# A state-space block on one core: sums over states and x*D turned in quarters of 32 channels, with one PSUM bank for each quarter

## The chip, the cores and the metric

The kernel runs on one core of a Trainium2 chip. The metric is the device time of one execution in microseconds (us); lower is better. Three executions of the kernel before took 2848.3, 2849.82 and 2853.23 us; their median, 2849.82 us, is what the changed kernel is compared with.

The engines have short names here: PE is TensorE's matmul row and PEld its weight loads, DVE is VectorE, ACT is ScalarE, POOL is GpSimd, and SP (SyncE) issues most of the DMAs.

## What is computed

The input x has 8 sequences of 2048 tokens of 512 channels, in fp32. A selective state-space layer with 16 states is added to x, and then a linear layer whose inputs are rounded to 8 bits. Cut to what matters:

```python
n = layernorm(x)
xp = n @ x_proj_w.T                       # 64 ranks, 16 B, 16 C
delta = softplus(xp[..., :64] @ dt_proj_w.T + dt_proj_b)
h[t] = exp(delta[t] * A) * h[t-1] + delta[t] * B[t] * n[t]   # per channel and state
y[t] = sum over the 16 states of h[t] * C[t]
x1 = x + y + n * D
z = layernorm(x1); zq = round(z / scale_of_row)
out = x1 + (zq @ weight_q.T) * scale_of_row * weight_scale + bias
```

## The kernel before, in words

The tokens are cut into 32 chunks of 512 (four chunks make one sequence). Within a chunk the kernel goes through 16 states, and within a state through the four groups `d` of 128 channels; one such step is a slot, so a chunk has 64 slots. Channels lie on the partitions while states are scanned along time, and tokens lie on the partitions before and after.

For each state of a chunk:

- ACT makes the decay `da` (line 742) and, for 10 of the 16 states, the product `bT` of delta*n with B, with tokens on the partitions (line 772). `b_pe` turns bT with transposes on PE (line 795). For the other six states a diagonal matrix with B on it is loaded from DRAM, and PE multiplies with it (line 786), which scales and turns at once.
- DVE runs the scan over 512 tokens, four to a state (line 804), reading `pb` from PSUM.
- POOL multiplies the state's result by C, 128 x 2048 elements in one instruction (line 830), giving `hc`.
- PE turns hc back to tokens and adds it to `y` in PSUM: `y_pe` and `y_halves` (lines 841 to 869). Each block of 128 channels x 128 tokens is turned as two products, one of partitions 0 to 63 and one of 64 to 127. In each, 64 rows of hc (128 columns) are the weights, and a 64 x 64 piece of the identity is the moving operand. A state has 16 blocks, so 32 such products.

Three things go into the same sums y. `skip_pe` (line 875) adds n*D with products against a diagonal of D, also in halves. `add_x` (line 580) adds the input x with the whole identity as weights, in two products of 256 columns. The state sums themselves accumulate over the whole chunk.

PSUM has eight banks. y takes four of them, as two tiles of two banks: tile `y0` holds token blocks 0 and 1, `y1` blocks 2 and 3. In each, one bank belongs to channel half 0 and the other to half 1, so that two products that run side by side write different banks. Three banks hold `pb` (tag "b") and one is for everything else (`misc`).

When a chunk's sums are complete, `residual` (line 611) copies y of each token block to SBUF on ACT (line 612), and the layer norm, the rounding and the quantized product of that chunk run in between the next chunk's states. y of the next chunk takes the same banks, so its first products wait for those copies.

The order on every engine is written out by hand. `pin` keeps instructions in program order, and `PREP_AT`, `POST_AT`, `LATE_AT`, `SKIP_AT` and `LAST_ADD_X` give a slot to each step. A chunk's last state sum stands in slot 7 of the next chunk, its last two add_x in slot 10, its four copies in slots 12, 12, 13 and 14, and the next chunk's first two state sums in slot 15. The transposes of bT run two slots ahead of the scans, bT and the decay about two states ahead. SP's queue carries the loads of x, of C (line 820) and of the diagonals (line 767).

At the start, 16 products of the identity with itself (line 507) keep PE working until the first tokens are normalised; then tokens are turned (line 456), projected (line 470) and taken to delta (lines 487 and 499), with `pdt` in the two y tiles. At the end, `finish` sums the last state channel group by channel group, copies y out (line 1003) and does the quantized product, with its output `po` (line 981) in the y tiles in turn.

Of the kernel before, what the change touches and what calls it, by code (L numbers as in the profile page):

```python
# [9 lines left out]
F32 = mybir.dt.float32  # L10
# [4 lines left out]
ALU = mybir.AluOpType  # L15
AX = mybir.AxisListType

P = 128
HALF = 64
T = 512  # L20
LN_EPS = 1e-05
Q_EPS = 1e-06
# [80 lines left out]
def kernel(  # L103
# [13 lines left out]
    nc = tc.nc  # L117
# [6 lines left out]
    ND = DM // P  # L124
    NT = T // P
    G = 4
    NG = N // G
    NPAIR = N // 2
    CPB = L // T
    NCHUNK = B * CPB  # L130
    assert OUT == T == DM

# [11 lines left out]
    ps_y = ctx.enter_context(tc.tile_pool(name="ps_y", bufs=1, space=bass.MemoryType.PSUM))  # L144
# [3 lines left out]
    pin = tc.keep_in_program_order  # L148
# [17 lines left out]
    ident = const.tile([P, P], F32, name="ident")  # L166
# [11 lines left out]
    pin(nc.sync.dma_start(out=dtproj_sb[:R], in_=dtproj_t))  # L178
    xp = const.tile([P, T], F32, name="xp")
    pin(nc.gpsimd.memset(xp, 0.0))  # L180
    dtb_sb = const.tile([P, ND], F32, name="dtb_sb")
    pin(nc.sync.dma_start(out=dtb_sb, in_=dt_b.rearrange("(c p) -> p c", p=P)))
    dsk_sb = const.tile([P, ND], F32, name="dsk_sb")
# [4 lines left out]
    pin(nc.sync.dma_start(out=wq_i32, in_=wq_t.rearrange("(c p) o -> p c o", p=P)))  # L188
    zeros = work.tile([P, T], F32, tag="hc", bufs=3, name="zeros")
    pin(nc.vector.memset(zeros, 0.0))  # L190
# [5 lines left out]
    diag_d = const.tile([P, ND, P], F32, name="diag_d")  # L196
# [23 lines left out]
    def gpsimd_constants():  # L220

        for d in range(ND):
            pin(
                nc.gpsimd.tensor_scalar(
                    diag_d[:, d, :], ident, dsk_sb[:, d : d + 1], None, ALU.mult
                )
            )
        pin(nc.gpsimd.tensor_copy(wq_sb, wq_i32.bitcast(I8)))
# [7 lines left out]
    das, pbs, bts, hs, hcs, ys = {}, {}, {}, {}, {}, {}  # L236
# [39 lines left out]
    def misc(name):  # L276
        return ps_m.tile([P, T], F32, tag="ps", name=name)

# [137 lines left out]
    def prep_first(second):  # L416
# [11 lines left out]
        bt = chan.tile([P, NT, N], F32, tag="BT", name="BT_0")  # L428
        b_t[0] = bt
        pts, pps = {}, {}  # L430

        def measure(i):
            st = small.tile([P, 6], F32, tag="st", name=f"st_0_{i}")
            pin(nc.vector.bn_stats(st, x[:, i, :]))
            pin(nc.vector.bn_aggr(mv[:, i, :], st))
            one = slice(i, i + 1)
            pin(nc.vector.tensor_scalar(ve[:, one], mv[:, i, 1:2], LN_EPS, None, ALU.add))
            pin(nc.gpsimd.tensor_tensor(rstd[:, one], ve[:, one], nhalf[:, one], ALU.pow))
# [41 lines left out]
        def dt(i):  # L480
            for d in range(ND):
                if i == 0:
                    if d % 2 == 0:
                        pdt = ps_y.tile([P, 2, T], F32, tag=f"y{d // 2}", name=f"pdt_0_{d // 2}")
                    pps[d] = pdt[:, d % 2, :]
                pin(
                    nc.tensor.matmul(
                        pps[d][:, ts(i, P)],
                        lhsT=dtproj_sb[:, ts(d, P)],
                        rhs=xp[:, ts(i, P)],  # L490
                        start=True,
                        stop=True,
                    )
                )
# [7 lines left out]
            )  # L502


        pw = misc("pwarm")
        for _ in range(16):
            pin(nc.tensor.matmul(pw[:, :P], lhsT=ident, rhs=ident, start=True, stop=True))
        measure(0)
        measure(1)
        norm(0)  # L510
# [44 lines left out]
        for s in range(2):  # L555
            bts[s] = work.tile([P, NT, P], F32, tag="dg", bufs=2, name=f"dg_0_{s}")
            for i in range(NT):
                pin(
                    nc.gpsimd.tensor_scalar(
                        bts[s][:, i, :], ident, bt[:, i, s : s + 1], None, ALU.mult  # L560
                    )
                )
        for d in range(ND):
# [4 lines left out]
            t = x[:, :, ts(d, P)]  # L568
            pin(nc.vector.tensor_tensor(t, pt.rearrange("p (i d) -> p i d", d=P), t, ALU.mult))
        b_pe(0)  # L570
        b_pe(1)
        plan(0, [(1, step) for step in second[3:]])
        gpsimd_constants()
        zero_diagonals(0)
        store_diagonals(0)
# [4 lines left out]
    def add_x(k, i):  # L580

        t = split(x1[k, i // 2][:, i % 2, :])
        for half in range(2):
            pin(
                nc.tensor.matmul(  # L585
                    ys[k, i // 2][:, half, i % 2, :, :],
                    lhsT=ident,
                    rhs=t[:, :, half, :],
                    start=False,
                    stop=False,  # L590
                    skip_group_check=True,
                )
            )

    def split(t):
        return t.rearrange("p (d h c) -> p d h c", h=2, c=HALF)

    def post(k):

# [241 lines left out]
    def y_pe(s):  # L841

        if s < 0 or s >= LAST - 1:
            return
        k, n = divmod(s, N)
        for i in range(NT):
            if n == 0 and i % 2 == 0:
                ys[k, i // 2] = ps_y.tile(  # L850
                    [P, 2, 2, ND, HALF], F32, tag=f"y{i // 2}", name=f"y_{k}_{i // 2}"
                )
            for d in range(ND):
                y_halves(k, i, d, hcs[s], first=(n == 0 and i % 2 == 0 and d == 0))

    def y_halves(k, i, d, hc, first=False, last=False):
        for half in range(2):
            rows = ds(half * HALF, HALF)
            pin(
                nc.tensor.matmul(  # L860
                    ys[k, i // 2][:, half, i % 2, d, :],
                    lhsT=hc[rows, d, ts(i, P)],
                    rhs=ident[rows, rows],
                    is_transpose=True,
                    start=first,
                    stop=last,
                    skip_group_check=True,
                )
            )

    def y_of(k, i):

        return ys[k, i // 2][:, :, i % 2, :, :].rearrange("p h d c -> p d h c")

    def skip_pe(k, i):

        for d in range(ND):
            for half in range(2):
                rows = ds(half * HALF, HALF)
                pin(  # L880
                    nc.tensor.matmul(  # L881
                        ys[k, i // 2][:, half, i % 2, d, :],
                        lhsT=xn_t[k][rows, d, ts(i, P)],
                        rhs=diag_d[rows, d, rows],
                        start=False,
                        stop=False,
                        skip_group_check=True,
                    )
                )

    def finish():


        k, s = NCHUNK - 1, LAST - 1
        h = hs.pop(s)
        hc = work.tile([P, ND, T], F32, tag="hc", bufs=3, name=f"hc_{k}_{N - 1}")
        c = cts.pop(s)
        for d in range(ND):
            pin(nc.vector.tensor_tensor(hc[:, d, :], h[:, d, :], c, ALU.mult))  # L899
            for i in range(NT):  # L900
                y_halves(k, i, d, hc, last=(d == ND - 1))
        mv = small.tile([P, NT, 2], F32, tag=f"mv{NT}", name="mv_last")
        am = small.tile([P, NT], F32, tag="am", name="am_last")
        xs = small.tile([P, NT], F32, tag="xs", name="xs_last")
# [8 lines left out]
        st = {}  # L913
# [27 lines left out]
        pw = misc("pwarm_last")  # L941
# [29 lines left out]
        def turned(i):  # L971
            qt = work.tile([P, ND, P], BF16, tag="qT", name=f"qT_last_{i}")
            pin(
                nc.scalar.activation(
                    qt,
                    st["pz", i].rearrange("p (d t) -> p d t", t=P),
                    AF.Copy,
                    bias=-ROUND,
                )
            )  # L980
            po = ps_y.tile([P, 2, T], F32, tag=f"y{i % 2}", name=f"po_last_{i}")[:, 0, :]
            for d in range(ND):
                pin(
                    nc.tensor.matmul(
                        po, lhsT=qt[:, d, :], rhs=wq_sb[:, d, :], start=(d == 0), stop=(d == ND - 1)
                    )
                )
            st["po", i] = po
# [23 lines left out]
        measure(3)  # L1012
        norm(2)
        turned(0)
        largest(1)
        rounded(1)
        norm(3)
        turned(1)
        for i in range(NT):
            pin(nc.gpsimd.tensor_tensor(x1_of(i), x1_of(i), bias_b, ALU.add))  # L1020
# [25 lines left out]
    for k in range(NCHUNK):  # L1046
        plan(k * SLOTS, [(SKIP_AT[i], lambda k=k, i=i: skip_pe(k, i)) for i in range(NT)])
        if k < NCHUNK - 1:
            plan((k + 1) * SLOTS, post(k))
        if k + 1 < NCHUNK:  # L1050
            plan(k * SLOTS, [at for at in prep_of[k + 1] if at[0] >= 0 or k > 0])
    want = 0
    for u in range(NCHUNK * SLOTS + Y_BEHIND):
        k, slot = divmod(u, SLOTS)
        s, d = divmod(u, ND)
# [28 lines left out]
        if k == NCHUNK - 1 and slot in LAST_LOAD:  # L1084
            j = LAST_LOAD.index(slot)
            t = work.tile([P, 2, DM], F32, tag="x1", bufs=3, name=f"x1_{k}_{j}")
# [53 lines left out]
```

## Time and profile before

| what | value |
|---|---|
| three executions | 2848.3, 2849.82, 2853.23 us |
| median | 2849.82 us |
| span of the profiled execution | 2848.6 us |
| instructions in it | 80379 |
| first chunk's stretch, 0 to 71 us: POOL busy | 44.60 us |
| line 860 weight loads | 16384, mean 139 ns |
| line 881, x*D | 2048 records, mean 275 ns |
| line 585, residual on PE | 512 records, mean 381 ns |
| ACT copies of y, line 612 | 124, median 588 ns |

The profile is of one execution. Its span of 2848.6 us runs from the first to the last instruction of the program; no other time is given for that execution, and it lies 1.2 us below the median.

In a row of the groups the columns are: line, engine, operation, output<-inputs, shapes and count, then busy time and mean duration in ns, then the idle time of the engine just before, and what ended it. A matmul's duration is from its start to a modelled end and includes the passage through the array; products overlap, so the distance between starts tells what one more product costs, and the busy time doesn't. An fp32 product that isn't a transpose has two records, for its two passes. In a timeline, rows of one group are merged: start, length of the whole group, and xN. A timeline of a narrow window counts the instructions that touch that window.

### The profile page before, as it was taken

How to read it: one execution, taken by the hardware profiler on the slowest of the kernel's cores; microseconds unless marked ns; L12 is line 12 of the kernel's file. 1: busy time of each engine (PE TensorE's matmuls, PEld its weight loads, DVE VectorE, ACT ScalarE, POOL GpSimd, SP SyncE). 2: the span in 40 equal slices, each digit the busy share in tenths (PEclk: the TensorE clock that was granted, in tenths of full speed). 3: DMA queues.
4: the chain of work that ended last, by engine and by line, in shares of the span. 5: the costliest groups of instructions: out<-in, count | busy, mean ns of one | idle time of the engine just before them, and what ended most of it. 6: DMA issues, size and time to landing. Idle time of an engine off the chain costs nothing.

```text
span 2848.6 us, 80379 instructions
## 1 busy us (share of the span) xinstructions
PE 2739.1 (96%) x33032; PEld 2357.2 (83%) x33032; DVE 2731.4 (96%) x2949; ACT 2723.7 (96%) x4762; POOL 2771.5 (97%) x1243
## 2 busy tenths in 40 slices
PE   8999999999999999999999999999999999999988
PEld 6888888888888888888888888888888878888877
DVE  6999999999999999999999999999999999999998
ACT  7999999999999999999999999999999999999995
POOL 6899999999999999999999999999999999999998
PEclk9999999999999999999999999999999999999999
DMA  5333343434434334444344343344444443434332
GB/s 151 107 92 95 106 113 109 109 80 105 113 109 116 87 97 110 106 117 105 85 106 111 109 118 85 101 109 106 116 104 89 106 109 109 111 81 102 100 99 71
DMA packets 260528, 295.90 MB, mean 104 GB/s; under 512 B 118144, under 2 KB 118656, under 8 KB 260160
## 3 DMA queue, kind: packets, MB, share of 16 engines
q1 hardware_dynamic: 259104, 290.53, 39.7%
q8 instruction: 259, 4.24, 0.6%
q14 instruction: 109, 0.89, 0.1%
q10 hardware_dynamic: 1056, 0.23, 0.0%
HBM read 252.55 MB, written 38.14 MB: 102 GB/s over the span
## 4 chain that ended last, share of the span: by engine, by line
PE 68%; DMA 9%; DVE 9%; ACT 5%; issue 4%; POOL 3%; SPq 1%; DVEq 0%; POOLq 0%; ACTq 0%
PE pb L786 22%; PE y L860 14%; PE pb L795 13%; DMA dg<-dg 8%; DVE h L804 7%; PE y L585 3%; PE po L677 3%; PE y L881 3%; PE pxp L311 2%; ACT da L742 2%; PE pdl L368 2%; POOL hc L830 2%; PE pz L660 2%; PE pxn L299 2%; ACT bT L772 2%
## 5 line engine op out<-in xcount | busy, mean ns | idle before, releaser
L804 DVE TENSOR_TENSOR_SCAN h<-da,pb 128x512 f32<-128x512 f32 x2048 | 2363.2, 1201 | 91.7 <-PE pb L786 51.7
L830 POOL TENSOR_TENSOR hc<-h,c 128x2048 f32<-128x2048 f32 x511 | 2328.1, 4563 | 20.2 <-DVE h L804 6.8
L742 ACT ACTIVATE da<-delta,a_neg 128x511 f32<-128x511 f32 (+1 forms) x2048 | 1381.8, 716 | 1.0 <-DVE h L804 0.6
L772 ACT ACTIVATE bT<-x,BT 128x512 f32<-128x512 f32 x1276 | 896.5, 715 | 0.0
L786 PE MATMUL pb<-dg,x 128*128 128x128 f32 x6176 | 785.6, 279 | 45.4 <-DMA dg<-dg 39.4
L786 PEld LDWEIGHTS pb<-dg,x 128*128 128x128 f32 x6176 | 739.2, 192 | 86.4 <-DVE h L804 45.5
L795 PE MATMUL pb<-ident,bT 128*128 128x128 f32 x5104 | 720.2, 276 | 23.6 <-DVE h L804 10.9
L795 PEld LDWEIGHTS pb<-ident,bT 128*128 128x128 f32 x5104 | 581.7, 141 | 183.8 <-issue 70.9
L860 PE MATMUL y<-ident,hc 64*128 64x64 f32 x16384 | 613.6, 226 | 1.9 <-DVE hc L899 1.0
L860 PEld LDWEIGHTS y<-ident,hc 64*128 64x128 f32 x16384 | 547.7, 139 | 75.4 <-issue 49.5
L242 DVE BATCH_NORM_STATS2 st<-x 128x6 f32<-128x512 f32 x244 | 156.3, 671 | 0.0
L350 PE MATMUL pdt<-xp,dtproj_sb 128*128 128x512 f32 x248 | 138.5, 640 | 11.9 <-ACT delta L360 11.4
L698 POOL TENSOR_TENSOR z<-z,x 128x1024 f32<-128x1024 f32 x62 | 147.6, 2380 | 0.0
L630 POOL TENSOR_TENSOR x<-x,bias_b 128x1024 f32<-128x1024 f32 x62 | 146.7, 2367 | 0.1
L881 PE MATMUL y<-diag_d,xnT 64*128 64x64 f32 x2048 | 138.7, 275 | 0.0
L881 PEld LDWEIGHTS y<-diag_d,xnT 64*128 64x128 f32 x2048 | 124.8, 188 | 10.7 <-issue 10.7
L677 PE MATMUL po<-wq_sb,qT 128*128 128x512 bf16 x496 | 127.6, 380 | 0.0
L360 ACT ACTIVATE delta<-pdt,dtb_sb 128x512 f32<-128x512 f32 x124 | 84.9, 685 | 44.6 <-PE pdt L350 43.7
L585 PE MATMUL y<-x,ident 128*128 128x256 f32 x512 | 127.4, 381 | 0.0
L311 PE MATMUL pxp<-xnT,xproj_sb 128*96 128x512 f32 x248 | 123.1, 598 | 0.0
L618 ACT ACTIVATE z<-x,nmr,rstd 128x512 f32<-128x512 f32 x124 | 97.1, 807 | 9.5 <-POOL nmr L258 9.5
L585 PEld LDWEIGHTS y<-x,ident 128*128 128x128 f32 x512 | 90.5, 192 | 8.6
(112 smaller groups left out, 1716.9 us busy)
## 6 DMA issues: line engine op xcount, KB each, us to landing
c<-bc SPq DMA_DIRECT2D x512, 256.0 KB, 3.5
dg<-dg SPq DMA_DIRECT2D x191, 256.0 KB, 4.7
x<-in_x_dram SPq DMA_DIRECT2D x64, 512.0 KB, 4.8
x<-in_x_dram SPq DMA_DIRECT2D x31, 1024.0 KB, 6.7
out_dram<-z SPq DMA_DIRECT2D x62, 512.0 KB, 4.6
dg<-zeros SPq DMA_DIRECT2D x12, 256.0 KB, 5.3
dg<-BT SPq DMA_DIRECT2D x192, 2.0 KB, 6.7
x<-in_x_dram SPq DMA_DIRECT2D x4, 256.0 KB, 4.4
```

Source lines behind the costliest of these rows:

```text
L242: pin(nc.vector.bn_stats(st, src))
L311: nc.tensor.matmul(st["pp"][:E], lhsT=xproj_sb[:, d, :], rhs=xn_t[k][:, d, :], start=(d == 0), stop=(d == ND - 1),)
L585: nc.tensor.matmul(ys[k, i // 2][:, half, i % 2, :, :], lhsT=ident, rhs=t[:, :, half, :], start=False, stop=False, skip_group_check=True,)
L677: nc.tensor.matmul(po, lhsT=qt[:, d, :], rhs=wq_sb[:, d, :], start=(d == 0), stop=(d == ND - 1))
L742: nc.scalar.activation(das[s][:, d, own], delta[k][:, d, own], AF.Exp, scale=a_neg[:, d, n : n + 1])
L772: nc.scalar.activation(bts[s][:, i, :], xn[k][:, i, :], AF.Copy, scale=b_t[k][:, i, n : n + 1])
L786: nc.tensor.matmul(pb[:, ts(i, P)], lhsT=xn[k][:, i, ts(d, P)], rhs=bts[s][:, i, :], start=True, stop=True,)
L795: pin(nc.tensor.transpose(pb[:, ts(i, P)], bts[s][:, i, ts(d, P)], ident))
L804: nc.vector.tensor_tensor_scan(hs[s][:, d, :], das[s][:, d, :], pbs.pop(u), 0.0 if k % CPB == 0 else 1.0, ALU.mult, ALU.add,)
L830: pin(nc.gpsimd.tensor_tensor(hc, h, c.unsqueeze(1).to_broadcast([P, ND, T]), ALU.mult))
L860: nc.tensor.matmul(ys[k, i // 2][:, half, i % 2, d, :], lhsT=hc[rows, d, ts(i, P)], rhs=ident[rows, rows], is_transpose=True, start=first, ...
L881: nc.tensor.matmul(ys[k, i // 2][:, half, i % 2, d, :], lhsT=xn_t[k][rows, d, ts(i, P)], rhs=diag_d[rows, d, rows], start=False, stop=Fals ...
```

## The change

The turning back of hc, and x*D, is done in quarters: four products of 32 channels for each block of 128, each with 32 rows of weights (still 128 columns) and a 32 x 32 piece of the identity, or of the diagonal of D. y becomes one tile of four banks, one bank for each quarter; all four token blocks lie in every bank. `add_x` becomes four products of 128 columns. What else lived in the y tiles (`pdt` at the start, `po` at the end) moves to one four-bank tile each. The warm-up products become 10 of 64 rows x 128 columns, 20 of 32 rows x 64 columns and 16 of 32 rows x 128 columns, into the same banks. Two scalings on GpSimd at the start get a second multiplication, by 1.0.

```diff
+QR = 32
+NQ = P // QR
...
-        pw = misc("pwarm")
-        for _ in range(16):
-            pin(nc.tensor.matmul(pw[:, :P], lhsT=ident, rhs=ident, start=True, stop=True))
+        pw = ps_y.tile([P, NQ, T], F32, tag="y", name="pwarm")
+        def warm_up(rows, cols, times):
+            for _ in range(times):
+                for g in range(P // rows):
+                    own = ds(g * rows, rows)
+                    pin(nc.tensor.matmul(pw[:, g, :cols], lhsT=ident[own, :],
+                                         rhs=ident[own, :cols], start=True, stop=True))
+        warm_up(HALF, P, 5)
+        warm_up(QR, HALF, 5)
+        warm_up(QR, P, 4)
...
-                        bts[s][:, i, :], ident, bt[:, i, s : s + 1], None, ALU.mult
+                        bts[s][:, i, :], ident, bt[:, i, s : s + 1], 1.0, ALU.mult, ALU.mult
...
     def add_x(k, i):
-        for half in range(2):
+        for q in range(NQ):
-                    ys[k, i // 2][:, half, i % 2, :, :],
+                    ys[k][:, q, i, :, :],
                     lhsT=ident,
-                    rhs=t[:, :, half, :],
+                    rhs=t[:, :, q, :],
...
-            if n == 0 and i % 2 == 0:
-                ys[k, i // 2] = ps_y.tile(
-                    [P, 2, 2, ND, HALF], F32, tag=f"y{i // 2}", name=f"y_{k}_{i // 2}"
-                )
+            if n == 0 and i == 0:
+                ys[k] = ps_y.tile([P, NQ, NT, ND, QR], F32, tag="y", name=f"y_{k}")
...
-    def y_halves(k, i, d, hc, first=False, last=False):
-        for half in range(2):
-            rows = ds(half * HALF, HALF)
+    def y_parts(k, i, d, hc, first=False, last=False):
+        for q in range(NQ):
+            rows = ds(q * QR, QR)
             pin(
                 nc.tensor.matmul(
-                    ys[k, i // 2][:, half, i % 2, d, :],
+                    ys[k][:, q, i, d, :],
                     lhsT=hc[rows, d, ts(i, P)],
                     rhs=ident[rows, rows],
                     is_transpose=True,
...
     def skip_pe(k, i):
         for d in range(ND):
-            for half in range(2):
-                rows = ds(half * HALF, HALF)
+            for q in range(NQ):
+                rows = ds(q * QR, QR)
...
-            po = ps_y.tile([P, 2, T], F32, tag=f"y{i % 2}", name=f"po_last_{i}")[:, 0, :]
+            if i == 0:
+                st["all"] = ps_y.tile([P, NT, T], F32, tag="y", name="po_last")
+            po = st["all"][:, i, :]
```

More of the change, by code (lines that the diff above doesn't have):

```diff
@@ L224, in gpsimd_constants @@
                 nc.gpsimd.tensor_scalar(
-                    diag_d[:, d, :], ident, dsk_sb[:, d : d + 1], None, ALU.mult
+                    diag_d[:, d, :], ident, dsk_sb[:, d : d + 1], 1.0, ALU.mult, ALU.mult
                 )
@@ L482, in dt @@
                 if i == 0:
-                    if d % 2 == 0:
-                        pdt = ps_y.tile([P, 2, T], F32, tag=f"y{d // 2}", name=f"pdt_0_{d // 2}")
-                    pps[d] = pdt[:, d % 2, :]
+                    if d == 0:
+                        pdt = ps_y.tile([P, ND, T], F32, tag="y", name="pdt_0")
+                    pps[d] = pdt[:, d, :]
                 pin(
@@ L502, in soft @@
             )
-        pw = misc("pwarm")
-        for _ in range(16):
-            pin(nc.tensor.matmul(pw[:, :P], lhsT=ident, rhs=ident, start=True, stop=True))
+        pw = ps_y.tile([P, NQ, T], F32, tag="y", name="pwarm")
[3 more added lines that the diff above has]
+                    own = ds(g * rows, rows)
+                    pin(
+                        nc.tensor.matmul(
+                            pw[:, g, :cols],
+                            lhsT=ident[own, :],
+                            rhs=ident[own, :cols],
+                            start=True,
+                            stop=True,
+                        )
+                    )
+        warm_up(HALF, P, 5)
+        warm_up(QR, HALF, 5)
+        warm_up(QR, P, 4)
         measure(0)
@@ L595, in split @@
     def split(t):
-        return t.rearrange("p (d h c) -> p d h c", h=2, c=HALF)
+        return t.rearrange("p (d q c) -> p d q c", q=NQ, c=QR)
     def post(k):
@@ L848, in y_pe @@
         for i in range(NT):
-            if n == 0 and i % 2 == 0:
-                ys[k, i // 2] = ps_y.tile(
-                    [P, 2, 2, ND, HALF], F32, tag=f"y{i // 2}", name=f"y_{k}_{i // 2}"
-                )
+            if n == 0 and i == 0:
+                ys[k] = ps_y.tile([P, NQ, NT, ND, QR], F32, tag="y", name=f"y_{k}")
             for d in range(ND):
-                y_halves(k, i, d, hcs[s], first=(n == 0 and i % 2 == 0 and d == 0))
-    def y_halves(k, i, d, hc, first=False, last=False):
-        for half in range(2):
-            rows = ds(half * HALF, HALF)
+                y_parts(k, i, d, hcs[s], first=(n == 0 and i == 0 and d == 0))
+    def y_parts(k, i, d, hc, first=False, last=False):
+        for q in range(NQ):
+            rows = ds(q * QR, QR)
             pin(
                 nc.tensor.matmul(
-                    ys[k, i // 2][:, half, i % 2, d, :],
+                    ys[k][:, q, i, d, :],
                     lhsT=hc[rows, d, ts(i, P)],
@@ L871, in y_of @@
     def y_of(k, i):
-        return ys[k, i // 2][:, :, i % 2, :, :].rearrange("p h d c -> p d h c")
+        return ys[k][:, :, i, :, :].rearrange("p q d c -> p d q c")
     def skip_pe(k, i):
         for d in range(ND):
-            for half in range(2):
-                rows = ds(half * HALF, HALF)
+            for q in range(NQ):
+                rows = ds(q * QR, QR)
                 pin(
                     nc.tensor.matmul(
-                        ys[k, i // 2][:, half, i % 2, d, :],
+                        ys[k][:, q, i, d, :],
                         lhsT=xn_t[k][rows, d, ts(i, P)],
@@ L900, in finish @@
             for i in range(NT):
-                y_halves(k, i, d, hc, last=(d == ND - 1))
+                y_parts(k, i, d, hc, last=(d == ND - 1))
         mv = small.tile([P, NT, 2], F32, tag=f"mv{NT}", name="mv_last")
```

## The prediction

> **What bounds the kernel now.** I read four views: the page, the busy time by windows, the waits, and the timeline of TensorE around one burst of line 860, narrowed until single weight loads could be told apart.
>
> ```profile
> span 2848.6 us, 80379 instructions
> ...
> PE 2739.1 (96%) x33032; PEld 2357.2 (83%) x33032; DVE 2731.4 (96%) x2949; ACT 2723.7 (96%) x4762; POOL 2771.5 (97%) x1243
> ...
> PE 68%; DMA 9%; DVE 9%; ACT 5%; issue 4%; POOL 3%; SPq 1%; DVEq 0%; POOLq 0%; ACTq 0%
> ...
> L830 POOL TENSOR_TENSOR hc<-h,c 128x2048 f32<-128x2048 f32 x511 | 2328.1, 4563 | 20.2 <-DVE h L804 6.8
> ...
> L795 PE MATMUL pb<-ident,bT 128*128 128x128 f32 x5104 | 720.2, 276 | 23.6 <-DVE h L804 10.9
> ...
> L860 PE MATMUL y<-ident,hc 64*128 64x64 f32 x16384 | 613.6, 226 | 1.9 <-DVE hc L899 1.0
> ```
>
> ```profile
> 1000.00:1500.00 500.00, 485.12 (x5864) 417.17 (x5862) 486.93 (x526) 486.06 (x843) 493.81 (x210) 1.00 0.41 103
> ```
>
> Four engines stand within two points of each other, so a share says little. The window (columns PE, PEld, DVE, ACT, POOL, clock) ranks them: in mid-run POOL works 493.8 us of 500, nearly all of it the product with C on line 830, whose 4563 ns this change doesn't touch. POOL is the pace. The chain of waits names TensorE for 68%, but it goes back through whatever came last, and TensorE feeds every scan; a matmul's recorded 226 to 276 ns is mostly its passage through the array, so 96% busy isn't 96% full.
>
> How full it is follows from start-to-start distances:
>
> ```profile
> 51.12 2.20 PE L860 MATMUL y<-ident,hc 64*128 64x64 f32 x64
> ```
> ```profile
> 1404.31 1.21 PE L860 MATMUL y<-ident,hc 64*128 64x64 f32 x32
> ```
> ```profile
> 1400.82 0.14 PEld L795 LDWEIGHTS pb<-ident,bT 128*128 128x128 f32 x1
> ```
> ```profile
> 1400.82 0.20 PEld L795 LDWEIGHTS pb<-ident,bT 128*128 128x128 f32 x2
> ```
> ```profile
> 1404.30 0.14 PEld L860 LDWEIGHTS y<-ident,hc 64*128 64x128 f32 x2 [0.17 <-issue]
> ```
> ```profile
> 1404.30 0.20 PEld L860 LDWEIGHTS y<-ident,hc 64*128 64x128 f32 x4 [0.17 <-issue]
> ```
> ```profile
> 1402.68 0.30 PEld L881 LDWEIGHTS y<-diag_d,xnT 64*128 64x128 f32 x4 [0.17 <-issue]
> ```
>
> Columns: start, length of the group. 32 more products of line 860 cost 2.20 - 1.21 = 0.99 us: 31 ns each, 62 ns for the two halves that make one 128x128 block. The two halves' weight loads start together (two take 0.14 us, as one does on line 795); the next two start 0.06 us later. On line 795, with all 128 rows, the second load also starts 0.06 us after the first. **So a load of 128 columns in transpose form blocks its rows for about 60 ns whether it fills 128 rows or 64**, and 62 ns a block is that price. On line 881 (ordinary fp32 products, two passes each) the step is 0.11 us.
>
> Adding up by such steps: L786 6176 x 112 ns = 692 us; L795 5104 x 109 = 556; L860 16384 x 31 = 508; L881 2048 x 56 = 115; L585 and L677 1008 x 215 = 217; L350 and L311 496 x 430 = 213; the other transposes 1488 x 109 = 162; small ones 12; entering and leaving some 540 bursts of half-height products at about 0.19 us (0.17 us stands as "issue" at each entry) about 100. Total 2575 us. TensorE has 273 us free, some 46 of them in the first and last chunk; the rest is **0.44 us for each of 512 states**. This is the cover for what the change adds.
>
> **The change part by part.**
>
> 1. *Sums over states (line 860).* 16384 products become 32768, four of 32 rows and 32 moving columns to a block. Each still loads 128 columns of hc. Bounds for a block, 62 ns now: from below 31 ns, if time goes with moving columns (half as many); from above 124 ns, if each product costs the 31 ns it shows now. I take **64 ns**, by the nearest row: the load's 60 ns doesn't depend on the row count where it can be seen, four row groups should load side by side as two do, and a few ns stand for two more starts. That the upper bound is not the cause of today's 62 ns speaks from the same rows: if products arrived one in 31 ns, the two halves would start 31 ns apart, and they start within 0.01 us. Sum: 16 x 2 = +32 ns a state. A burst ends with 32 moving columns instead of 64: 276 - 226 = 50 ns for 64 columns (L795 against L860), so -25 ns. Net +7 ns, **+4 us of TensorE in all**; bounds 16 x -31 = -0.50 and 16 x +62 = +0.99 us a state.
>
> A rule of the Trainium skill, "TensorE: Matmul & The Clock Gate", section "LDWEIGHTS (loading the stationary operand)", speaks against this change: a weight load's time goes with its columns, 32 rows costing what 128 do. The trace agrees for 64 against 128 rows (0.06 us both) and doesn't show 32; the page's formula gives 107 ns for 128 columns where 60 ns is measured, and the measurement decides. The same page, in "Wait — 56ns, not 53.3ns?", has starts never closer than about 25 ns. The halves' starts within 0.01 us contradict that across row groups; were it right for four, a block would take an estimated 100 ns and the run about 2970 us.
>
> 2. *x*D (line 881).* 2048 records become 4096. Now 16 records take eight steps of 0.11 us; in quarters, eight steps of four loads each: 0. Bounds: -0.44 us a call (half the steps) and +0.89 (twice), over 128 calls -57 and +114 us of TensorE. I take 0, by the same load row.
>
> 3. *Residual by TensorE (line 585).* Two products of 256 columns become four of 128, two passes each: 4 x 0.215 = 0.86 us becomes 8 x 0.112 = 0.90 (step of L786): +0.04 x 128 = +5 us of TensorE.
>
> 4. *One four-bank tile for two of two banks.* The four copies of line 612 used to need only their own pair of banks; now every token block lies in every bank, and the changed program's instruction order shows a new wait on TensorE at each chunk's first copy. It must wait for all of add_x:
>
> ```profile
> 916.67 1.46 PE L585 MATMUL y<-x,ident 128*128 128x256 f32 x6
> ...
> 917.23 1.05 ACT L612 COPY x<-y 128x512 f32<-128x512 f32 x2
> ```
>
> Here the copy starts 0.90 us before add_x ends, so it is late by that. Over 31 chunks such overlaps add up to about 13 us of ACT, most of it in two chunks. Behind the copy on ACT stand exponentials and bT pieces for two states ahead; ACT has 500 - 486 = 14 us free in 500. Hidden, except perhaps +1 us; all 13 without cover. In the other direction, the next chunk's first sums now wait for the fourth copy, not the second. In this profile that copy ends at least 0.5 us before those sums start, and usually about 1 us: nothing, or +0.5 x 31 = +16 us if ACT slips further.
>
> 5. *Start.* 16 warm-up products (32 records, 6.26 us) become 46 (92 records). With row groups side by side 14 products' length counts for 16: 5.5 us, and the first real transpose, at 7.48 us right behind them, gains at most 0.6 us, since its input is ready at 6.88. One after another they would take 46/16 x 6.26 = 18 us: +12 us at most. I take 0. The extra multiply by 1.0 on GpSimd touches 12 instructions before POOL's first product and none after: 0, at most their own 7 us again.
>
> 6. *End.* po has four banks, so the last two output products no longer wait for the first two to be read: 0 to -1 us.
>
> 7. *Instruction fetch.* 17694 more products in the program; the instruction queue's 0.6% of DMA time becomes about 1%. The diagonal loads on the chain (8%) run beside it: 0 to +3 us.
>
> TensorE gains about +9 us of work under a cover of 227. DVE's waits for pb (51.7 + 24.8 us) grow by a like share, 9/227 = 4%, or 3 us, of which POOL passes on a part. I put the sum at **+2 us** on the span. The span lies 1.2 us under the median of 2849.82, so the forecast is 2848.6 + 2 + 1.2 = 2852.
>
> **Rivals.**
>
> *Quarters pass at the moving columns' rate* (31 to 55 ns a block). For: columns per product halve. Against: the 0.06 us load step. TensorE frees 0.1 to 0.5 us a state, but POOL keeps its pace: beyond its steady 0.5 us a chunk it idles some 22 us in mid-run. Gain 5 to 24 us: 2826 to 2845.
>
> *Issue becomes the bound* (the other side). Twice as many instructions pass one sequencer; if they pass no faster than now, a block takes 124 ns and a state gains 0.99 us against 0.44 free. TensorE takes over the pace once a block passes 62 + 440/16 = 90 ns; just below that its stalls already show. At 124 the sum is 2575 + 508 + 46 at the ends and about 40 for waits on diagonals = 3170. At 75 to 90 ns most of the cover is eaten: 2860 to 2900. For: nothing in the trace shows more than four TensorE instructions in 62 ns. Against: the halves' simultaneous starts.
>
> *The change does nothing in mid-run*, since the same loads set the same block time: my forecast, 2844 to 2866.
>
> **How the numbers follow.** Neutral (55 to 75 ns a block) 0.65; moving-column rate 0.11; partly issue-bound (75 to 90) 0.09; issue-bound beyond that 0.15. A measurement of this kernel can tell about 0.2%, 5.7 us. Of the neutral case 0.41 lies within that, 0.18 slower by add-ons of parts 4, 5 and 7, 0.06 faster. Faster 0.06 + 0.11 = 0.17; same 0.41; slower 0.18 + 0.09 + 0.15 = 0.42. The neutral case alone spans 2844 to 2866; the range runs from the moving-column case to the end of the partly issue-bound one, 2826 to 2900, leaving out the issue-bound case.
>
> **What would show it.** Right: a 64-product burst about 1.0 us first to last as the 32-product one is now, four starts within 0.02 us, and POOL near 494 of 500. Moving-column rate: bursts near 0.55 us, mid-run waits of DVE for pb shrinking. Issue-bound: starts spread evenly, bursts up to 2 us, DVE waiting for pb in every state, POOL under 480. Part 4: a wait of ACT before L612's first copy. Part 5: the first pxn transpose later than 7.48 us. I'd be wrong above all if four row groups don't load side by side.

## The result, and the profile after

The changed kernel took 2866.97 us (median of four executions, 2863.84 to 2872.52) beside 2849.76 us (2848.3 to 2853.23) for the kernel before, whose executions are now four: a ratio of 1.0067, 95% interval 1.0049 to 1.0085. It is slower by about 17 us, median against median. Run twice more, in other sets of runs beside other kernels, it came to 1.0023 (1.0011 to 1.0035) and 1.0046 (1.0029 to 1.0063): slower each time, by an amount that changes from set to set.

The page of the changed kernel, profiled in an execution with a span of 2867.5 us:

```profile
span 2867.5 us, 118320 instructions
...
PE 2735.7 (95%) x51912; PEld 2385.4 (83%) x52036; DVE 2731.1 (95%) x2949; ACT 2722.3 (95%) x4762; POOL 2769.7 (97%) x1243
...
q8 instruction: 407, 6.67, 1.0%
...
PE 62%; ACT 17%; DVE 8%; DMA 6%; issue 4%; POOL 2%; SPq 1%; DVEq 0%; POOLq 0%; ACTq 0%
...
L822 DVE TENSOR_TENSOR_SCAN h<-da,pb 128x512 f32<-128x512 f32 x2048 | 2364.7, 1201 | 108.9 <-PE pb L813 49.4
L848 POOL TENSOR_TENSOR hc<-h,c 128x2048 f32<-128x2048 f32 x511 | 2331.0, 4568 | 24.0 <-DVE h L822 11.8
...
L876 PE MATMUL y<-ident,hc 32*128 32x32 f32 x32768 | 603.2, 223 | 5.5 <-issue 4.0
```

TensorE's products on line 876 have doubled in number and take no more time (603.2 us; 613.6 before), as forecast. POOL's product costs the same. What has grown is DVE's wait for `pb` of line 813 (49.4 us; 24.8 before, line 795); its wait for line 804, the products with diagonals, has come down (40.4 us; 51.7 before, line 786), so the two together went from 76.5 to 89.8 us. The timeline of TensorE around single bursts of line 876 shows the price of a block; columns are start and length of the group:

```profile
623.95 1.18 PE L876 MATMUL y<-ident,hc 32*128 32x32 f32 x64
...
661.18 2.18 PE L876 MATMUL y<-ident,hc 32*128 32x32 f32 x128
...
623.95 0.20 PEld L876 LDWEIGHTS y<-ident,hc 32*128 32x128 f32 x8
```

64 more products cost 1.00 us, 62 ns for the four that make a block, as two halves did. Eight loads fit in the 0.20 us in which the halves showed four. In the records the first four products start within 10 ns. So far the step the forecast rested on holds, and the time is still longer. Two things stand out in the timeline. One is a place that comes once in nearly every chunk, behind the burst of state 5, ahead of the last softplus:

```profile
1209.37 1.18 PE L876 MATMUL y<-ident,hc 32*128 32x32 f32 x64
...
1210.48 1.12 PE L352 MATMUL pdt<-xp,dtproj_sb 128*128 128x512 f32 x2
...
1211.45 0.60 PE L813 MATMUL pb<-ident,bT 128*128 128x128 f32 x4
...
1213.53 0.69 ACT L362 ACTIVATE delta<-pdt,dtb_sb 128x512 f32<-128x512 f32 x1 [2.92 <-PE pb L813]
1213.59 1.22 DVE L822 TENSOR_TENSOR_SCAN h<-da,pb 128x512 f32<-128x512 f32 x1 [0.94 <-remote]
...
1214.27 2.08 PE L352 MATMUL pdt<-xp,dtproj_sb 128*128 128x512 f32 x2 [2.22 <-ACT delta L362]
...
1216.14 1.06 PE L813 MATMUL pb<-ident,bT 128*128 128x128 f32 x4
```

The product that the softplus reads ends at 1211.60 by the record, and ACT starts at 1213.53, 1.9 us later; where nothing else holds it, it starts 0.04 us after. I call such a signal **late**: TensorE's semaphore event comes over 0.1 us after the modelled end (13 to 22 ns is usual). There is one such event in the kernel before, of 0.45 us. Here there are 73, 84.6 us in all, up to 2.9 us each, all at this place, while `store_diagonals` writes 3072 pieces of 4 bytes, or just after it. Whether the product itself or only its signal is late, these records don't tell.

The other is in the same lines: after the gap line 352 takes 2.08 us instead of 1.12 and line 813 1.06 instead of 0.60. The busy time by windows has the reason in its column PEclk, behind POOL's:

```profile
1000.00:1500.00 500.00, 481.41 (x9078) 417.89 (x9100) 480.63 (x522) 479.62 (x831) 488.00 (x207) 0.99 0.40 104
...
1210.60:1214.10 3.50, 1.45 (x6) 0.68 (x6) 2.56 (x3) 0.58 (x2) 3.50 (x2) 0.99 0.87 81
1214.10:1217.50 3.40, 3.23 (x9) 2.09 (x10) 0.97 (x2) 2.01 (x5) 3.40 (x3) 0.50 0.89 134
1893.30:1896.70 3.40, 1.82 (x77) 1.67 (x70) 3.40 (x7) 1.89 (x4) 3.40 (x3) 1.00 0.04 13
1896.70:1900.10 3.40, 3.40 (x12) 2.26 (x11) 2.93 (x4) 3.26 (x7) 3.40 (x1) 0.50 0.23 75
```

TensorE runs at half clock for one window of 3.41 us after a window with a gap. Between 45 and 2730 us there are six such windows here, and two in the kernel before (in two kernels below one stretch at half clock lasted two windows, 6.83 us; it counts as one). The second in the kernel before was:

```profile
2307.10:2310.50 3.40, 1.03 (x8) 0.62 (x7) 3.40 (x5) 3.40 (x8) 3.40 (x3) 1.00 0.90 302
2310.50:2313.90 3.40, 3.40 (x12) 3.04 (x13) 1.91 (x3) 3.06 (x6) 3.40 (x2) 0.50 0.36 132
```

The page's row PEclk is 9 in every slice of both kernels: slices of 70 us are too coarse to show it.

### The profile page after: what moved, and what is told of

The parts are those of the page before. It is cut to its first block, busy times and chain, and to the rows that moved or that the text cites. A ratio compares the mean times of both kernels' runs of the same rounds, so it can differ in the third digit from the quotient of the medians.

```text
span 2867.5 us, 118320 instructions
## 1 busy us (share of the span) xinstructions
PE 2735.7 (95%) x51912; PEld 2385.4 (83%) x52036; DVE 2731.1 (95%) x2949; ACT 2722.3 (95%) x4762; POOL 2769.7 (97%) x1243
## 4 chain that ended last, share of the span: by engine, by line
PE 62%; ACT 17%; DVE 8%; DMA 6%; issue 4%; POOL 2%; SPq 1%; DVEq 0%; POOLq 0%; ACTq 0%
PE pb L804 18%; PE pb L813 13%; PE y L876 12%; ACT da L760 8%; DVE h L822 6%; ACT bT L790 5%; DMA dg<-dg 4%; PE y L603 3%; PE pdt L352 3%; PE y L897 3%; PE po L695 2%; PE pxp L313 2%; PE pdl L370 2%; PE pz L678 2%; PE pxn L301 2%
## 5 line engine op out<-in xcount | busy, mean ns | idle before, releaser
L822 DVE TENSOR_TENSOR_SCAN h<-da,pb 128x512 f32<-128x512 f32 x2048 | 2364.7, 1201 | 108.9 <-PE pb L813 49.4
L804 PE MATMUL pb<-dg,x 128*128 128x128 f32 x6176 | 786.3, 279 | 27.6 <-DMA dg<-dg 25.0
L876 PEld LDWEIGHTS y<-ident,hc 32*128 32x128 f32 x32768 | 549.4, 137 | 79.4 <-issue 55.5
L876 PE MATMUL y<-ident,hc 32*128 32x32 f32 x32768 | 603.2, 223 | 5.5 <-issue 4.0
L897 PE MATMUL y<-diag_d,xnT 32*128 32x32 f32 x4096 | 138.1, 272 | 0.0
L897 PEld LDWEIGHTS y<-diag_d,xnT 32*128 32x128 f32 x4096 | 127.7, 188 | 10.7 <-issue 10.7
L603 PE MATMUL y<-x,ident 128*128 128x128 f32 x1024 | 130.2, 275 | 0.0
L695 PE MATMUL po<-wq_sb,qT 128*128 128x512 bf16 x373 | 121.1, 380 | 6.5
L603 PEld LDWEIGHTS y<-x,ident 128*128 128x128 f32 x1024 | 122.1, 192 | 0.1
L774 POOL TENSOR_TENSOR da<-first_a,state 128x4 f32<-128x4 f32 x384 | 85.0, 221 | 19.8 <-DVE h L822 9.7
```

Of the source, the lines that this page charges most:

```text
L603: nc.tensor.matmul(ys[k][:, q, i, :, :], lhsT=ident, rhs=t[:, :, q, :], start=False, stop=False, skip_group_check=True,)
L695: nc.tensor.matmul(po, lhsT=qt[:, d, :], rhs=wq_sb[:, d, :], start=(d == 0), stop=(d == ND - 1))
L804: nc.tensor.matmul(pb[:, ts(i, P)], lhsT=xn[k][:, i, ts(d, P)], rhs=bts[s][:, i, :], start=True, stop=True,)
L822: nc.vector.tensor_tensor_scan(hs[s][:, d, :], das[s][:, d, :], pbs.pop(u), 0.0 if k % CPB == 0 else 1.0, ALU.mult, ALU.add,)
L876: nc.tensor.matmul(ys[k][:, q, i, d, :], lhsT=hc[rows, d, ts(i, P)], rhs=ident[rows, rows], is_transpose=True, start=first, stop=last, ski ...
L897: nc.tensor.matmul(ys[k][:, q, i, d, :], lhsT=xn_t[k][rows, d, ts(i, P)], rhs=diag_d[rows, d, rows], start=False, stop=False, skip_group_c ...
```

## The experiments

**Theory A**: the late signals cost the time. **Theory B**: the half-clock windows cost it, whatever opens the gap before them. **Theory C**: the new warm-up starts the clock later. Part 4, the one tile, is tried by itself. The expectations of experiments 1 to 4 were written before B and C in this sense: there, B is the one tile, and C more work on TensorE. All kernels of a set ran beside the kernel before, so ratios are compared.

*1. The changed kernel without the writes of the diagonals*

```diff
             b_t[k] = t
-            store_diagonals(k)
```

> The changed kernel without the six small writes of each later chunk's diagonals (their products then use stale diagonals; only the first chunk's are written). Theory A, late completions: in the changed profile the products of state 5 of each chunk signal their end 0.5 to 2.9 us late, just where these writes of 4 bytes each are under way, and the third softplus waits for it. Then without the writes no softplus should start more than 0.1 us after its product in mid-run for this reason, ACT's wait for pb before softplus (37.9 us) should be gone, and the time should fall by some 14 to 20 us, to about 2847 to 2853. Theory B, one tile: ACT's new wait at the copies costs the 17 us; the writes don't matter, and the time stays at 2860 or more. Theory C, TensorE's own work grew: also 2860 or more.

*2. The kernel before without them* (same edit)

> The kernel before without the same writes, to tell what they cost by themselves. Theory A: no late signals there to lose, so 2843 to 2850, and the ratio of e1 to this one is 1.000 to 1.003. Theories B and C: the ratio of e1 to this one stays near 1.006.

Measured: 1.0034 (1.0021 to 1.0047) for the changed kernel, 0.9996 (0.9987 to 1.0005) for the kernel before; median against median 2853.21 / 2841.31 = 1.0042, between the 1.000 to 1.003 of A and the 1.006 of its rivals. The late signals are gone, all 73. But 11.9 us of difference are left, and five half-clock windows stand in mid-run, at other places than the six above, one behind this pair (window by window, the clock is the third column from the end):

```profile
485.40:488.80 3.40, 1.78 (x112) 1.67 (x104) 3.40 (x7) 2.57 (x5) 3.40 (x3) 1.00 0.20 72
488.80:492.20 3.40, 3.40 (x14) 2.96 (x15) 2.17 (x3) 2.12 (x5) 3.40 (x1) 0.50 0.33 82
```

So A is right that the signals are late only with the writes, and can't be the whole cause. Whether the time came down at all isn't shown by this run: with the writes, the changed kernel came to 1.0023 and 1.0046 in its other sets.

*3. Only state 5's burst in another order, quarters 0 and 1 of all blocks, then 2 and 3*

```diff
+        if n == 5:
+            for qs in ((0, 1), (2, 3)):
+                for i in range(NT):
+                    for d in range(ND):
+                        y_parts(k, i, d, hcs[s], qs=qs)
```

> The changed kernel with one state sum of sixteen, that of state 5, written in another order: all blocks' quarters 0 and 1, then all blocks' quarters 2 and 3. Two row groups run side by side instead of four, with the same 64 products; this burst lasts about 2 us instead of 1, so TensorE gets 1 us more work in each chunk and half as many products per us in this one place. Theory A, in the form that the rate of ending products beside the writes is what matters: the late signals go (under 0.1 us) or fall under a third, and the time falls to 2850 to 2858. If the form of 32 rows or four banks itself makes them late, they stay as they are and the time is 2866 to 2885. Theories B and C: 2866 to 2885.

Measured: 1.0052 (1.0037 to 1.0067); 35 late signals, 28.8 us in all, and one half-clock window. Two row groups at a time are late less often and by less. The time doesn't tell this from the changed kernel, but this burst now takes 1.74 us from its first start to its last instead of 0.96, in each chunk, so the run doesn't price the signals.

*4. The kernel before, in halves, with one four-bank tile*

```diff
-            if n == 0 and i % 2 == 0:
-                ys[k, i // 2] = ps_y.tile(
-                    [P, 2, 2, ND, HALF], F32, tag=f"y{i // 2}", name=f"y_{k}_{i // 2}")
+            if n == 0 and i == 0:
+                whole = ps_y.tile([P, 2, 2, 2, ND, HALF], F32, tag="y", name=f"y_{k}")
+                ys[k, 0], ys[k, 1] = whole[:, 0], whole[:, 1]
```

> The kernel before, in halves, with its two y tiles made into one of four banks (each bank as before holds one half of two token blocks); pdt and po move as in the change. Theory B, one tile: 2860 to 2867, with ACT waiting at the copies. Theory A: 2848 to 2853, no late signals. Theory C: the same as A here.

Measured: 1.0015 (1.0004 to 1.0027), 1 to 8 us; the one tile isn't the 17 us. Among the waits of ACT is the new one (us in total, times, longest):

```profile
ACT x L612 <- PE y L585: 14.0, 8, 7.3
```

7.3 us of it is at the copies of the last chunk but one, where the kernel of experiment 2 waits too (6.5 us, for POOL); in mid-run some 7 us of ACT are left, nearly half of it in one chunk (3.0 us at 2045 us, just behind this profile's one half-clock window, at 2041 us). The wait is there, with the size the forecast bounded.

*5 to 8. The changed kernel with the stores moved from slot 26 to slot 36 or 29, with the old warm-up, and unchanged*

```diff
-            store_diagonals(k)
...
+        once["stores"] = lambda: store_diagonals(k)   # PREP_AT: stores=36, or stores=29
```

> The changed kernel with the six transfers that store the next chunk's diagonals handed out at slot 36 in place of slot 26. Theory A (a burst of 64 quarter products is told as ended late while these transfers' 4-byte writes are under way): the late signals leave state 5's burst (slot 31) and the third softplus, which starts 0.04 us after its product again, and turn up at state 7's burst (slot 39), again by up to 3 us; the time stays within 0.3% of the changed kernel's. Rival theory (it is the place: the burst of state 5 is late because three softplus products and the step product stand around it, whatever is stored): the late signals stay at state 5's burst, up to 2.9 us, in some 29 of 31 chunks.

> The changed kernel with the same six transfers handed out at slot 29, so that their 4-byte writes fall mostly between the bursts of two states. Theory A: few late signals or none (under 15 us in all, against 84.6 us in the changed kernel), and the time near that of the run without the stores, 1.003 times the kernel before. Rival theory (the place, not the writes): as many late signals as in the changed kernel, 1.005 to 1.0067 times the kernel before.

> The changed kernel with the 16 whole-array warm-up products of the kernel before. Theory C1 (row-tiled warm-up products bring TensorE's full clock later): full clock by 7 us (6.49 us before, 9.15 us after), the first scan at 22.2 us (22.21 before, 23.65 after); if that lasts to the end, 1.4 us or 0.05% is won. Rival (the start is caught up by the first chunk's other work): the first scan is earlier by 1.4 us, the end of the first chunk is not, and the time is the changed kernel's within 0.05%.

> The changed kernel itself beside the three others, on the same chip. All theories: 1.005 to 1.0085 times the kernel before; late signals at state 5's burst in most chunks, some 85 us in all; half-clock windows of 3.4 us in the middle of the run in about 6 places, at other places than in the first profile if they depend on small differences of timing.

Measured, with the half-clock windows between 45 and 2730 us of each profile:

| kernel | ratio to before (95%) | late signals | half-clock windows |
|---|---|---|---|
| stores at 36 | 1.0035 (1.0025 to 1.0045) | 22, 16.8 us | 3 |
| stores at 29 | 1.0057 (1.0038 to 1.0077) | 57, 52.9 us | 5 |
| old warm-up | 1.0019 (1.0009 to 1.0029) | 57, 48.8 us | 2 |
| unchanged | 1.0023 (1.0011 to 1.0035) | 54, 58.5 us | 1 |

With the stores at 36 the late signals leave state 5's burst and follow the writes, to scan slots 36 and 37 (state 6's burst, not state 7's as I had expected). At 29 the writes moved less than meant: they still fill scan slots 29 to 33, so that run separates nothing, though what it showed is what the rival had forecast. As the main cause of the time, A falls here: the unchanged kernel has 58.5 us of late signals at 1.0023, and experiment 1 has none at 1.0034. The number of half-clock windows orders the four ratios except for the two lowest, which are equal within their intervals. That is weak support for B: a count is of one execution, for the unchanged kernel of the fastest of its ten (2846.41 us; median 2850.94), and experiment 3, with one window at 1.0052, doesn't fit the order.

Theory C: the old warm-up takes 5.68 us, then the first turn of x starts at 6.90:

```profile
1.38 5.68 PE L509 MATMUL pwarm<-ident 128*128 128x128 f32 x32 [1.38 <-POOL ident masks.py:199]
6.90 0.60 PE L458 MATMUL pxn<-ident,x 128*128 128x128 f32 x4
```

In the changed kernel's profile:

```profile
1.39 6.66 PE L514 MATMUL pwarm<-ident 64*128 64x128 f32 x92 [1.39 <-POOL ident masks.py:199]
7.97 1.65 PE L458 MATMUL pxn<-ident,x 128*128 128x128 f32 x8
```

Full clock comes at 5.28 us against 9.65 in the unchanged kernel, the first scan at 22.55 against 23.65, and the second chunk's first scan is 1.5 us earlier. Whether any of that lasts isn't shown: over the 14 profiles this second chunk starts between 112.5 and 115.8 us, in the kernel before, with the old warm-up, at 114.8. It would be some 0.05%, less than these ratios can tell.

**Theory F** came out of the same traces. At the double burst of chunks 5 and 21 (128 products in a row) the quarter kernels pause for 1 to 2 us inside the burst, with no releaser but "issue". In the first profile of the changed kernel:

```profile
1893.78 0.62 PE L876 MATMUL y<-ident,hc 32*128 32x32 f32 x27
1895.97 0.24 PE L876 MATMUL y<-ident,hc 32*128 32x32 f32 x1 [1.58 <-issue]
1896.15 0.66 PE L301 MATMUL pxn<-ident,x 128*128 128x128 f32 x4
```

A fetch of 16384 bytes on the instruction queue is under way from 1893.60 to 1894.54, and of 87 pauses inside a burst (over 0.3 us from one start to the next) in the ten profiles in quarters, 86 have one under way within 1.6 us ahead of them or during them (by chance some 40% would, with 407 fetches of about 1 us). The four profiles in halves have no such pause. So F says: TensorE runs out of instructions. That is argued from where the pauses stand; no run here tests it alone.

*9 to 12. Filler products that raise the streaming time, in both kernels*

```diff
+    def filler(k):     # 512 columns, zero weights, onto the last quarter's bank
+        nc.tensor.matmul(ys[k][:, NQ - 1, :, :, :], lhsT=dtproj_sb[HALF:, :P],
+            rhs=ident[HALF:, :].unsqueeze(1).to_broadcast([HALF, NT, P]),
+            start=False, stop=False, skip_group_check=True)
...
+            if d == 0 and k >= 2: filler(k - 2)    # behind xnt_pe(0), slot 9
+            if d == ND - 1: filler(k - 1)          # ahead of dt_pe(3), slot 32
...
                 y_pe(sy - 1)
+                filler(sy // N)                    # the fourth run only, slot 15
```

> The changed kernel with two filler products a chunk, each 512 columns with zero weights added onto the last quarter's bank (nothing is added to the sum): one behind the first turn of x at slot 9, one ahead of the fourth step product at slot 32, the two places where TensorE's idle time of 1.2 to 2.3 us precedes most half-clock windows. Theory B (a window of 3.41 us in which columns stream for less than some 0.4 of the time is followed by one at half clock, and that costs 2 to 3 us): no half-clock window at slots 9, 10, 33 and 34, at most the two at slot 16; the time is below that of the changed kernel on the same chip by 2 to 3 us for each window that goes, so 0 to 14 us. Rival A (the late signals next to the small writes cost the time, the clock only follows): late signals as in the changed kernel, and the time the same or longer, by up to 25 us if the fillers' 0.85 us each are not hidden (31 chunks of 0.85 us).

> The kernel before with the same two fillers (in the bank of its second half). Theory B: its rare half-clock windows in the middle of the run (two at 426 and 2310 us in the first profile, at slots 34 and 10) go too; 0.998 to 1.000 times the kernel before. If the fillers are not hidden: up to 1.01.

> The changed kernel itself beside these, since its ratio was 1.0067 on one chip and 1.0023 on another. Theory B: more half-clock windows in the middle of the run than the kernel before shows (it had two), and the ratio follows their number: 1.002 with one or two, 1.005 or more with five or six. Rival A: the ratio follows the sum of the late signals (84.6 us with 1.0067, 58.5 us with 1.0023).

> The changed kernel with the two fillers, a third between the turns of state 0 and state 1 (slot 15, inside the double burst of 128 products), and the 16 whole-array warm-up products of the kernel before. Theory F (TensorE's instructions run out in the dense burst: a fetch of 16 KB lands just before the 1.3 to 1.8 us pauses inside the double burst of chunks 5 and 21): the filler gives the fetch time, the pauses inside the double burst go, and with them the last half-clock windows at slot 16. With B and F together the time comes to 1.000 to 1.002 times the kernel before, what the one four-bank tile costs (1.0015); if it stays at 1.003 or more, something else is left.

| kernel | ratio to before (95%) | late signals | half-clock windows |
|---|---|---|---|
| changed, two fillers | 1.0158 (1.0143 to 1.0173) | 60, 50.4 us | 2 |
| before, two fillers | 1.0116 (1.0101 to 1.0132) | 0 | 0 |
| changed, unchanged | 1.0046 (1.0029 to 1.0063) | 59, 54.0 us | 3 |
| changed, three fillers, old warm-up | 1.0262 (1.0247 to 1.0277) | 59, 58.5 us | 0 |

The clock did what B expected of the fillers, but there was little to remove: of the three windows of the unchanged kernel beside them one stood at these slots (215 us), the others in double bursts. With fillers none of the half-clock windows left stands at slots 9, 10, 33 or 34; the two in the first of these kernels follow pauses within a burst, one of them here:

```profile
693.52 0.94 PE L892 MATMUL y<-ident,hc 32*128 32x32 f32 x47
695.84 0.44 PE L892 MATMUL y<-ident,hc 32*128 32x32 f32 x17 [1.38 <-issue]
```

But the fillers were not hidden, and no time was won: I expected at most 14 us less, and the fourth run at 1.000 to 1.002. In the kernel before they cost 2873.10 - 2841.19 = 31.9 us, 0.52 us for each of 61 fillers of 0.85 us (two passes of 0.43 us); in the changed kernel 33.6 us. So about 0.33 us of a filler was free there. The third filler, at slot 15, added 2913.40 - 2885.80 = 27.6 us with the old warm-up, 0.86 us for each of 32, its whole length. These runs agree with B on what brings the half-clock windows, and don't show what the windows cost. No version here that does the whole work beats the kernel before.

**What the windows cost.** That I take from the chunks. For chunks 1 to 29 of 11 profiles (all kernels above but those with fillers) I subtracted from each chunk's length that of the same chunk in experiment 2's profile, which has no half-clock window, no pause and no late signal there, and fitted the rest to what the trace shows in that chunk. A half-clock window goes with 2.12 us (standard error 0.11), a microsecond of pause within a burst with 0.57 us (0.08), a microsecond of late signals with 0.095 us (0.025), and the quarter form by itself with -0.10 us (0.08). For the first two profiles:

| chunks 1 to 29, after less before | us |
|---|---|
| four more half-clock windows x 2.12 | 8.5 |
| 80 us more of late signals x 0.095 | 7.6 |
| 5.7 us of pauses x 0.57 | 3.2 |
| the form itself, 29 x -0.10 | -3 |
| sum | 16 |
| measured | 16.9 |

This is a fit over traces, not an experiment: late signals open some of the gaps before the windows, so the two share their part. In the first profile four of the six windows stand behind such a gap, one behind a wait of 2.21 us for the load of a diagonal (at 1305.69 us), and one behind a pause.

There is a second measure, since the record has the granted clock of every execution, to 0.001. One window of 3.41 us at half clock lowers the mean of 2850 us by 0.0006. In the 52 executions of the kernel before, in the last three sets (its profile shows a single late signal), the slower ones have the lower clock (correlation -0.64 within the sets), with 1.3 us (error 0.2) for each window's worth of clock. Over all 135 executions, each kernel by itself, it is 1.0 us (error 0.1). This too is a correlation. By it the 2.12 us of the fit seem to hold part of what opens the gap. The unchanged kernel had 0.0015 and 0.0020 less clock than the kernel before in its last two sets, an estimated 2.5 and 3.4 windows. At 1.0 to 1.3 us that is 3 to 4 us of the 7 and 11 us between the medians; at 2.12, 5 to 7. What makes up the rest stays open.

**What brings a window.** I counted for each window of 3.41 us how long moving columns stream, at 0.83 ns an fp32 column (512 columns of line 350 step in 0.43 us; bf16 half of that). Over 14 profiles and away from both ends: of 19 windows with a share under 0.35, 18 were followed by half clock; of 83 from 0.35 to 0.50, 13; of about 10,700 above, none. The largest idle time of TensorE in or at the end of those 31 was a wait for a diagonal's load in 11 (both of the kernel before), a pause within a burst in 13, a softplus behind a late signal in 4, and none of these in 3. A block in halves streams for 53 of its 62 ns, in quarters for 27. The mean share fell from 0.84 to 0.76, so the same gap should bring the window around it closer to the bound; that the quarters made the windows more frequent in this way, beside the new gaps, is argued and not tested.

## Why the prediction was right or wrong, point by point

- **Step 1** (64 ns a block, TensorE +4 us): right; 62 ns, the last of 64 products 0.96 us after the first. Four row groups do load side by side. Clean chunks of the quarter form are no longer than those in halves (-0.10 us, error 0.08): both of the rivals built on the block time fall. POOL's sign, near 494 us of 500, failed in the first profile (488.0, with three half-clock windows in that stretch) and came in the two later ones of the same kernel (495.7 and 495.3).
- **Step 2** (x*D, 0): right; 138.1 us busy beside 138.7. **Step 3** (add_x, eight steps of 0.112 us): right, the step is 112 ns.
- **Step 4** (+1 us, at most 13 us of ACT): the wait and its size are as described; alone it cost 1 to 8 us, so +1 stands at the lower end. How 7 us of ACT in mid-run become some 4 us of time isn't settled.
- **Step 5** (start 0, bounds -0.6 to +12): inside the bounds, though its sign of being wrong came: the first turn of x starts at 7.97 us instead of 7.48, since the warm-up took 6.66 us and not 5.5. The first scan came 1.1 us later than with the old warm-up. **Step 6** (end): not to be seen. From the last chunk's start to the end the changed kernel took 119.0, 117.8 and 118.5 us in three profiles, the kernel before 115.9, and without stores 119.1.
- **Step 7** (0 to +3 us, by loads of diagonals beside the fetches): the size, 3.2 us by the fit, is at the bound; the way was another. TensorE itself pauses in its densest bursts, while its waits for loads of diagonals were shorter than before (25.0 us; 39.4 before).
- **The cover** ("0.44 us for each of 512 states"): not tested as a mean. A filler of 0.85 us at slots 9 and 32 cost 0.52 us on average, so 0.33 us were free there, somewhat less than the mean. The change hardly drew on it, since its bursts cost nothing more.
- **The sum** (+2 us; measured +17, and in the other two sets 0.23% and 0.46%, 7 and 11 us by the medians): this is the step that failed. It put DVE's waits for pb at 3 us more, and they grew by 13. It has no term for TensorE's clock and none for the late signals. The window that I read, 1000 to 1500 us, showed a clock of 1.00; the kernel before had its two half-clock windows outside of it. That a quarter streams half as long was in the forecast only as a possible gain. The slower side had its largest chance, with other reasons. That 2866.97 us lies inside the range of 2826 to 2900 is partly luck: it is just above the 2844 to 2866 of the case that came, blocks of 62 ns, and and the range reaches past it only to cover a partly issue-bound case that didn't come.

A rule of the Trainium skill pointed at the clock. "TensorE: Matmul & The Clock Gate", section "What's actually happening", says that the clock falls to half after an idle window of 3413 ns, and that these windows run freely. The runs agree on the windows: the half-clock windows of each profile lie on one grid of 3.413 us, to within 5 ns. On "idle" they differ: windows in which columns streamed for nearly half of the time were followed by half clock too, mostly with a gap of only 1.0 to 2.2 us.

## What to carry to other kernels

Going from two row groups to four left the price of a block as it was here (62 ns), doubled the instructions and halved the time in which columns stream; look at the sparsest stretches of 3.4 us, not at a mean clock, before thinning TensorE's work. Spare time on an engine is worth what it is at the place where work is added: a filler put in by itself measures that (0.33 us of 0.85 was free at two places here, nothing at a third). A difference that moves from 0.2% to 0.7% between sets of runs is likely made of events, so count the events in several profiles, and compare the clock of all executions, before one of them is named the cause; the most visible one here, the late signals, was not the whole of it.

## What the runs showed of the hardware that was not expected

- Signals of TensorE come up to 3 us late when a burst of 64 products in four row groups stands beside about 3000 DMA writes of 4 bytes: 54 to 73 times in a run with the writes in their place or nearly so, 22 times with them some six slots later, 35 times with two row groups at a time in that burst, never without them, and once in the four profiles in halves. Why stays open, and so does whether the product or the signal is late.
- 128 products in four row groups with their loads, 256 instructions in 2 us, pause beside a fetch of instructions at some places of the program (0.3 to 2.0 us from one start to the next; with the new warm-up and no filler always in the double burst of chunk 5 and, but for the reordered kernel, of chunk 21); 64 products in halves in the same time never did. That TensorE outruns the fetch is the likely reading, not a tested one. That a filler of 0.85 us inside the double burst gives the fetch time was not cleanly tested: with it no pause stood there, but it also shifted the program.
- Row-tiled warm-up products bring the full clock later: at 8.9 to 14.3 us in eight profiles, against 5.3 to 7.4 us in the six with whole-array products.
